# Layer 3's products inside layer 2: source tiles 13 to 48 in batches of eight, 18 dense node tiles, all count matrices made by step 256

## The chip, the cores and the metric

The kernel runs on one core of a Trainium2 chip. The metric is the device time of one execution in microseconds. Before the change it is 3082.79 us, the median of three runs (3079.99 to 3087.31 us). All times below belong to one execution that the hardware profiler recorded; that one took 3087.14 us.

## The reference: what is computed

A graph network of four layers runs over 6,250 nodes with 256 features and 100,000 edges, and its result is added to the input. `src` is random; `dst` is sorted and crowded at low node numbers (the square of a uniform variable), so node 0's neighbourhood has many more edges than node 6,249's.

```
h = relu(layernorm(x))
h = h @ W1_self + mean(h[src] by dst) @ W1_neigh + b1
hp = relu(h @ W2_pool + b2_pool)
h = h @ W2_self + max(hp[src] by dst) @ W2_neigh + b2
h = ((sum(h[src] by dst) + h) / (deg + 1)) @ W3_neigh + b3
h = h @ W4_self + mean(h[src] by dst) @ W4_neigh + b4
out = x + h @ W_fc + b_fc
```

Weight matrices that follow one another are multiplied together in the kernel, so that layers 3 and 4 are sums over edges, with scalings.

## The kernel before, in words

Nodes are cut into 49 tiles of 128 rows (P = 128); edges into T = 782 steps of 128. The work lies in `fast_path`; `general_path` stands behind an `If` that is not taken for these inputs.

**Sums over edges, in two ways.** For node tiles with many edges ("dense" tiles: the first 8 in layer 1, 16 in layer 3, 18 in layer 4; `HUB = (8, 16, 18)`, in the code H1, H3, H4) the kernel has a count matrix: for destination tile d and source tile s, how often each source row reaches each destination row, as fp8 numbers. `dense` (L424) multiplies it with the source rows, which are held as three bf16 parts in turn: three matmuls for each pair (d, s) (L435). For the other node tiles, `sums` (L360) gathers 128 source rows for each edge step by an indirect DMA on GpSimd's queue (L379), and multiplies them with a one-hot matrix (three matmuls, L397). Layer 3 gathers from the edge step at which tile H3 can begin: 342 steps with H3 = 16 (314 with 18, as layer 4 has it). The dense work is handed out evenly over these steps through a `Hub`, a list of work items of which `advance` runs so many.

**Count matrices.** `build` (L291) makes one from 128-edge rows. For each item ScalarE makes one one-hot matrix (two activations, L303 and L305), VectorE another (L307), TensorE multiplies them (L313), ScalarE copies the sum into the tile `A` (L317), of which there is one (`bufs=1`); after each tile's 32 items SyncE writes `A` (784 KB) to the table `tab_a` (L321). Tiles 0 to 7 are made in layer 1, tiles 8 to 17 during layer 2.

**Layer 2** is a running maximum over all 782 edge steps, in six blocks of steps taken from the last to the first (100, 130, 180, 220, 100, 52 steps). Each step: one gather of 128 rows of 2 KB from `tab_p` on GpSimd's queue (L1137), a VectorE maximum with the row before (L1142), for every second step a write of the result to `runb` by SyncE (L1183). In the last three blocks a second maximum merges two rows (L1178), and half as much is written. There are six buffers of two steps each for `X`. At the end of each block `carry` joins the partial maxima across partitions (L1006 to L1040): gather, maximum, scatter; only then are the node tiles of this block finished by `done2` (L1055), from tile 48 down to tile 0, spread over the steps: it gathers the maxima (`totals`, `tot`, at most 4 buffers), waits for four steps, then makes transposes, eight fp32 matmuls (L1070 to L1076), the sum `prf` (L1080), and splits it into three bf16 parts `r3` (L280 to L283), which SyncE writes to `tab_r`, layer 3's table.

**Layer 3's products inside layer 2.** While the parts of tile d are still on chip, the kernel uses them for layer 3's dense sums: `EARLY = (6, 38)` says for which source tiles, `BATCH = 4` how many are taken at once. `early_products` (L1099) makes for each batch and each of the H3 dense tiles one load of the counts (`ae`, 64 KB, SyncE, L1108) and one group of 4 x 3 matmuls of 512 columns into a PSUM bank (`psd`, 2 banks); then `add3` (L931) adds the bank to an fp32 accumulator in SBUF on VectorE (L934; the first time a ScalarE copy, L937). The source tiles outside this range are done in layer 3 from tiles `zt` that are loaded from `tab_r` when that stage opens (`late`, three loads, 17 source tiles).

**The order.** The Python loop at L1128 to L1200 hands out the work step by step (`at` counts the steps): so many builds, so many items of early work, one piece of each open `done2`. Within that order of priority the compiler's scheduler places instructions in each engine's queue; each engine then runs its own queue in order. Builds of tiles 8 to 15 are spread up to step 250, those of 16 and 17 from there to step 682. Early work runs at a fortieth of what is left, rounded up, at each step; tile 37 to 34's batch is the first and is handed over at step 307.

```
early.advance(early.done + math.ceil(early.left() / 40))
if tiles and not ends and begun2 < NT * (at - FIRST_AT) / (T - 20 - FIRST_AT):
```

Of the kernel before, what the change touches and what calls it, by code (L numbers as in the profile page):

```python
# [10 lines left out]
BF16 = mybir.dt.bfloat16  # L11
F16 = mybir.dt.float16
F8 = mybir.dt.float8e4
# [7 lines left out]
P = 128  # L21
# [6 lines left out]
MERGED = 3  # L28
Z_SIGMA = 5.0
WIN = 8  # L30
HUB = (8, 16, 18)
EARLY = (6, 38)
MADE_AT = 64
FIRST_AT = 112
EARLY_AT = 250


def _edges_below(n, E, N):
# [35 lines left out]
def fast_path(  # L74
# [18 lines left out]
    FH = W1_self.shape[1]  # L93
    FO = W_fc.shape[1]
    NT = (N + P - 1) // P
# [3 lines left out]
    T = (E + P - 1) // P  # L99
# [11 lines left out]
    for d in range(NT):  # L111
# [4 lines left out]
        g_of.append((g0, g1))  # L116
    JC = g_of[HUB[0]][0] * G // P
    offs = [0]
# [13 lines left out]

    H1, H3, H4 = HUB
    WT = P // WIN
# [80 lines left out]
    at = 0  # L215
# [110 lines left out]
    LOOK = 4  # L326
# [195 lines left out]
    RB1 = -(-(max(row_of[w, k] for w in range(WT * H1) for k in range(k_of[w])) + 1) // P) * P  # L522
# [275 lines left out]
    with ExitStack() as on:  # L798
# [3 lines left out]
        psb = on.enter_context(tc.tile_pool(name="psb1", bufs=2, space=PSUM))  # L802
        psd = on.enter_context(tc.tile_pool(name="psd1", bufs=2, space=PSUM))
        wk = on.enter_context(tc.tile_pool(name="fl1", bufs=2))
# [4 lines left out]
        def done1(d, acc):  # L809
# [23 lines left out]
            for k in range(KI):  # L833
# [12 lines left out]
                        lambda acc, d=d: todo.append(done1(d, acc)), extra=1)  # L846
                  for d in range(H1)]
        work = list(builds[0])
        first = len(work)
        for d in range(H1):  # L850
            work += merged(denses[d], builds[d + 1]) if d + 1 < H1 else denses[d]
        hub = Hub(work)
# [86 lines left out]
    with tc.tile_pool(name="fl2c", bufs=1) as ck, ExitStack() as late:  # L939
# [3 lines left out]
        psb = late.enter_context(tc.tile_pool(name="psb2", bufs=2, space=PSUM))  # L943
# [4 lines left out]
        skR = ck.tile([P, RB * P - RB1], F32, name="skR")  # L948
        mkR = ck.tile([P, RB * P - RB1], F32, name="mkR")
# [52 lines left out]
        wk = late.enter_context(tc.tile_pool(name="fl2", bufs=2))  # L1002
# [51 lines left out]

        def done2(d):  # L1055
            tots, th = totals(d)
            for _ in range(4):
                yield
            hm = tots[0]
            for t in tots[1:]:  # L1060
                nc.vector.tensor_tensor(hm, hm, t, op=ALU.max)
            yield
            pt = bank(pst, "pt", "pt_hTf", (KH, P))
            for j in range(KH):
                nc.tensor.transpose(pt[:, j, :], hm[:, j * P : (j + 1) * P], ident)
            hT = wk.tile([P, KH, P], F32, name="hTf")
            nc.scalar.copy(hT, pt)  # L1067
            pm = bank(psm, "pm", "pm_prf")
            for k in range(KI):
                nc.tensor.matmul(pm, th[:, k, :], usA[:, k, :], start=(k == 0), stop=False)  # L1070
            yield
            for k in range(KI):
                nc.tensor.matmul(pm, th[:, KI + k, :], usB[:, k, :], start=False, stop=False)
            yield
            for c in range(KH):
                nc.tensor.matmul(pm, hT[:, c, :], un[:, c, :], start=False, stop=(c == KH - 1))  # L1076
                if c == 1:
                    yield
            pr = wk.tile([P, FH], F32, name="prf")
            nc.vector.tensor_add(pr, pm, prow)  # L1080
            yield
            if d < H3:
                add3(d, pr)
            r3 = early_pool[0].tile([P, 3 * FH], BF16, name="r3", bufs=2 * BATCH + 1)
            parts(pr, FH, r3)
            nc.sync.dma_start(tab_r[d * P : (d + 1) * P, :], r3)
            if EARLY[0] <= d < EARLY[1]:
                ready.append((d, r3))
                if len(ready) == BATCH or d == EARLY[0]:
                    early_products()  # L1090
            yield


        BATCH = 4
        ready = []
        early = Hub()
        early_pool = []

        def early_products():  # L1099
            batch = dict(ready)  # L1100
            ss = sorted(batch)
            ready.clear()
            for d in range(H3):
                got = {}

                def load(d=d, got=got):
                    got[0] = early_pool[0].tile([P, BATCH, P], F8, name="ae", bufs=LOOK + 3)
                    nc.sync.dma_start(got[0][:, : len(ss), :].bitcast(BF16),  # L1108
                                      tab_a[d, :, ss[0] : ss[-1] + 1, :])

                work = dense(ss, lambda s, got=got: got[0][:, s - ss[0], :],
                             lambda s: batch[s], FH, psd, lambda v, d=d: add3(d, v))
                early.add([(load, work[0])] + work[1:])
# [2 lines left out]
        todo = [chains(), node_rows(wk, psm)]  # L1116
        steps = products2(wpool)
        A = wk.tile([P, NT, P], F8, name="A", bufs=1)
        first, rest = (
            [w for d in ds for w in build(d, A, (skR, mkR, RB1), wk, psb)]  # L1120
            for ds in (range(H1, H3), range(H3, H4))
        )
        hub = Hub(first + rest)
        tiles, begun2 = [], 0
        ends = []
        now = []
        at = 0
        for b in reversed(range(NB)):  # L1128
            tb = BLOCKS[b]
            t0 = offs[b] // P  # L1130
            prev = None
            for s0 in range(0, tb, G2):
                n = min(G2, tb - s0)
                X = (xmore if at // G2 % 2 else xpool).tile([P, G2, FH], F32, name="X2")
                for k in range(n):
                    t = t0 + s0 + k
                    nc.gpsimd.indirect_dma_start(  # L1137
                        out=X[:, k, :], out_offset=None, in_=tab_p,
                        in_offset=bass.IndirectOffsetOnAxis(ap=srcI[:, t : t + 1], axis=0),
                    )  # L1140
                    if s0 + k:
                        nc.vector.scalar_tensor_tensor(  # L1142
                            X[:, k, :], prev, same[:, t : t + 1], X[:, k, :],
                            op0=ALU.mult, op1=ALU.max,
                        )
                    prev = X[:, k, :]
                    at += 1
                    if at > 8:
                        next(steps, None)
                        if todo and next(todo[0], 0) == 0:  # L1150
                            todo.pop(0)
                    if at == MADE_AT:
                        for _ in steps:
                            pass
                        top.close()
                        early_pool.append(
                            top.enter_context(tc.tile_pool(name="early3", bufs=1)))
                    if at <= EARLY_AT:
                        hub.advance(math.ceil(len(first) * max(0, at - 16) / (EARLY_AT - 16)))
                    else:  # L1160
                        hub.advance(len(first) + math.ceil(
                            len(rest) * (at - EARLY_AT) / (T - 100 - EARLY_AT)))
                    early.advance(early.done + math.ceil(early.left() / 40))
                    if s0 + k > 2 and ends and next(ends[0], 0) == 0:
                        ends.pop(0)
                        tiles += [d for d in reversed(range(NT)) if b_of[d][0] == last_b]
                    if tiles and not ends and begun2 < NT * (at - FIRST_AT) / (T - 20 - FIRST_AT):
                        now.append(done2(tiles.pop(0)))
                        begun2 += 1
                    for g in list(now):  # L1170
                        if next(g, 0) == 0:
                            now.remove(g)
                r0 = s0
                if b < MERGED:
                    r0 = s0 // 2
                    if s0 + n < tb:
                        t = t0 + s0 + 1
                        nc.vector.scalar_tensor_tensor(  # L1178
                            X[:, 0, :], prev, same[:, t : t + 1], X[:, 0, :],
                            op0=ALU.mult, op1=ALU.max,  # L1180
                        )
                        n = 1
                nc.sync.dma_start(  # L1183
                    runs[b][r0 * P : (r0 + n) * P, :].rearrange("(g p) f -> p g f", p=P),
                    X[:, :n, :],
                )
            end = carry(b, prev)
            next(end)
            ends.append(end)
            last_b = b  # L1190
# [49 lines left out]
    with ExitStack() as on:  # L1240
# [2 lines left out]
        psm = on.enter_context(tc.tile_pool(name="psm3", bufs=2, space=PSUM))  # L1243
        zk = on.enter_context(tc.tile_pool(name="fz4", bufs=1))
        Z4 = {}
        z4_early = ((16, 23), (23, 30), (30, 37))
        z4_late = ((0, 7), (7, 14), (14, 16), (37, 44), (44, NT))

        with tc.tile_pool(name="fl3", bufs=2) as wk:
            def done3(d, acc):  # L1250
# [33 lines left out]
                    if d == s1 - 1:  # L1284
                        Z4.update(resident(zk, tab_s, FO, s0, s1))

            late = ((EARLY[1], 44), (44, NT), (0, EARLY[0]))
            Z3 = {}
            for s0, s1 in late:
                Z3.update(resident(wk, tab_r, FH, s0, s1))  # L1290
# [3 lines left out]
            for d in range(H3):  # L1294
                work += dense([s for s0, s1 in late for s in range(s0, s1)], lambda s, d=d: block(d, s), lambda s: Z3[s], FH, psd,
                              lambda acc, d=d: todo.append(done3(d, acc)))
            sums(wk, psg, tab_r, FH, srcE, keyE, jb, H3, done3, 7, Hub(work), wait=14, todo=todo)

        with tc.tile_pool(name="fl4", bufs=2) as wk:
# [15 lines left out]
            for d in range(H4):  # L1315
                work += dense([s for s0, s1 in order for s in range(s0, s1)],
                              lambda s, d=d: block(d, s), lambda s: Z4[s], FO, psd,
                              lambda acc, d=d: todo.append(done4(d, acc)))
# [644 lines left out]
```

## Time and profile before

| | us |
|---|---|
| median of three runs | 3082.79 |
| the profiled execution | 3087.14 |
| its span on the core | 3085.3 |
| start of layer 2's gathers | 821.0 |
| last of layer 2's gathers | 2105.5 |
| last write of `tab_r`, layer 3 opens | 2139.64 |
| loads of `zt` for layer 4, which opens | 2647.1 |

TensorE is busy for 2456.4 us of the span (80%), VectorE 2053.6 (67%), GpSimd 2054.0 (67%), ScalarE 893.7 (29%); the DMA engines move 865.38 MB. Such shares are means over four stages that have different limits; a row of the stage view gives the busy time of each engine (and in brackets its instructions) in one stretch, the share of full clock that TensorE was granted, and the busy share of the 16 DMA engines. A DMA share of about 1 means that they had no free time. A row of a group of instructions gives its line, engine, operands, number, busy time, mean length, and after the bar how long its engine stood idle just before it and for whom. Back-to-back matmuls overlap in their recorded lengths, so their rate is read from a run of several.

### The profile page before, as it was taken

How to read it: one execution, taken by the hardware profiler on the slowest of the kernel's cores; microseconds unless marked ns; L12 is line 12 of the kernel's file. 1: busy time of each engine (PE TensorE's matmuls, PEld its weight loads, DVE VectorE, ACT ScalarE, POOL GpSimd, SP SyncE). 2: the span in 40 equal slices, each digit the busy share in tenths (PEclk: the TensorE clock that was granted, in tenths of full speed). 3: DMA queues.
4: the chain of work that ended last, by engine and by line, in shares of the span. 5: the costliest groups of instructions: out<-in, count | busy, mean ns of one | idle time of the engine just before them, and what ended most of it. 6: DMA issues, size and time to landing. Idle time of an engine off the chain costs nothing. (4 is left out here: it accounts for less than half of the span.)

```text
span 3085.3 us, 41397 instructions
## 1 busy us (share of the span) xinstructions
PE 2456.4 (80%) x12699; PEld 1401.4 (45%) x12699; DVE 2053.6 (67%) x5303; ACT 893.7 (29%) x2383; POOL 2054.0 (67%) x2260
## 2 busy tenths in 40 slices
PE   1568999999768555666789997972899899799997
PEld 0234666666433222232334443431344344688786
DVE  4955666655367677555789997974466667576665
ACT  2557766664255566311111111000000001000000
POOL 5274777776366776777667777764676677677663
PEclk9777999999889777788899998985999999899999
DMA  5454667776599999999989998976999999777774
GB/s 190 152 159 138 203 208 211 213 217 211 196 392 376 362 388 352 362 389 384 314 274 324 315 309 296 323 248 210 361 387 373 364 386 382 254 225 219 208 210 135
DMA packets 379984, 865.38 MB, mean 280 GB/s; under 512 B 58064, under 2 KB 151202, under 8 KB 379720
## 3 DMA queue, kind: packets, MB, share of 16 engines
q0 software_dynamic: 146560, 514.74, 50.7%
q1 hardware_dynamic: 175108, 292.47, 25.6%
q10 hardware_dynamic: 58084, 55.44, 5.6%
q8 instruction: 103, 1.69, 0.2%
q14 instruction: 129, 1.06, 0.1%
HBM read 610.65 MB, written 252.58 MB: 280 GB/s over the span
## 5 line engine op out<-in xcount | busy, mean ns | idle before, releaser
L1137 POOL DMA_INDIRECT X<-tab_p,srcIf x782 | 842.3, 1077 | 368.6 <-issue 170.5
L397 PE MATMUL pg<-ring,hot 128*128 128x256 bf16 (+2 forms) x3390 | 685.9, 311 | 96.2 <-DMA ring<-tab_h,srcT 36.5
L435 PE MATMUL pd<-zt,ac 128*128 128x256 bf16 (+1 forms) x3462 | 569.9, 300 | 36.3 <-DMA ac<-tab_a 31.1
L379 POOL DMA_INDIRECT ring<-tab_h,srcT x474 | 450.7, 951 | 194.3 <-PE pg L397 72.2
L397 PEld LDWEIGHTS <-hot 128*128 128x128 bf16 x3390 | 334.2, 99 | 332.1 <-issue 163.4
L435 PE MATMUL pd<-r,ae 128*128 128x512 bf16 x1536 | 383.4, 399 | 102.9 <-DVE acc L934 46.9
L379 POOL DMA_INDIRECT ring<-tab_r,srcE x342 | 333.0, 974 | 162.2 <-PE pg L397 72.5
L435 PEld LDWEIGHTS <-ac 128*128 128x128 fp8e4 x3462 | 338.8, 98 | 171.3 <-DMA ac<-tab_a 23.9
L379 POOL DMA_INDIRECT ring<-tab_s,srcE x314 | 297.7, 948 | 130.2 <-PE pg L397 49.4
L1142 DVE SCALAR_TENSOR_TENSOR X<-X,samef,X 128x512 f32<-128x512 f32 x385 | 288.3, 749 | 133.2 <-DMA X<-tab_p,srcIf 90.9
L416 DVE SCALAR_TENSOR_TENSOR acc<-pg,M,acc 128x257 f32<-128x257 f32 (+2 forms) x518 | 274.7, 561 | 150.6 <-PE pg L397 150.3
L1142 DVE SCALAR_TENSOR_TENSOR X<-X,samef 128x512 f32<-128x512 f32 x391 | 293.1, 750 | 114.2 <-DMA X<-tab_p,srcIf 108.0
L313 PE MATMUL pb<-hm,hs 128*128 128x392 bf16 x781 | 256.2, 376 | 132.4 <-ACT A L317 66.4
L305 ACT ACTIVATE hs<-ht,onef 128x128 bf16<-128x128 bf16 x781 | 290.2, 395 | 240.9 <-PE pb L313 221.9
L435 PEld LDWEIGHTS <-ae 128*128 128x128 fp8e4 x1536 | 156.4, 102 | 338.9 <-issue 198.8
L1219 DVE TENSOR_SCALAR_CACHE_REDUCE many<-ac 128x896 bf16<-128x896 fp8e4 (+2 forms) x144 | 138.7, 963 | 132.7 <-DMA ac<-tab_a 132.7
L1076 PE MATMUL pm_prf<-unf,hTf 128*128 128x512 f32 x392 | 203.9, 647 | 16.6 <-ACT hTf L1067 16.6
L375 DVE TENSOR_SCALAR hot<-iota_bf,keyE 128x128 bf16<-128x128 bf16 x656 | 151.2, 274 | 72.5 <-PE pg L397 65.4
L307 DVE TENSOR_SCALAR hm<-iota_w,mk 128x392 bf16<-128x392 f16 x461 | 155.2, 344 | 56.7 <-PE pb L313 55.0
L317 ACT ACTIVATE A<-pb 128x392 fp8e4<-128x392 f32 x288 | 139.8, 489 | 182.0 <-PE pb L313 137.7
L435 PE MATMUL pd<-Z,A 128*128 128x256 bf16 (+1 forms) x1176 | 187.4, 274 | 0.2
L313 PEld LDWEIGHTS <-hs 128*128 128x128 bf16 x781 | 81.4, 105 | 217.7 <-issue 89.2
(288 smaller groups left out, 2908.1 us busy)
## 6 DMA issues: line engine op xcount, KB each, us to landing
runb<-X SPq DMA_DIRECT2D x208, 512.0 KB
runb<-X SPq DMA_DIRECT2D x183, 256.0 KB
tab_r<-r SPq DMA_DIRECT2D x49, 384.0 KB
tab_a<-A SPq DMA_DIRECT2D x18, 784.0 KB
tab_t<-th SPq DMA_DIRECT2D x49, 256.0 KB
tab_p<-hpf SPq DMA_DIRECT2D x49, 256.0 KB
th<-tab_t ACTq DMA_DIRECT2D x49, 256.0 KB
X<-tab_p,srcIf POOLq DMA_INDIRECT x782
```

What stands on the lines that cost most here:

```text
L305: nc.scalar.activation(hots[0], t, AF.Relu, bias=one, scale=-1.0)
L307: nc.vector.tensor_scalar(hots[1], iota_w, mk[:, r : r + 1], None, op0=ALU.is_equal)
L313: nc.tensor.matmul(hold[0], hots[0], hots[1], start=(k == 0), stop=(k == k_of[w] - 1))
L317: nc.scalar.copy(A[:, :, c : c + WIN], hold[0].rearrange("p (s c) -> p s c", c=WIN), saturate=True)
L375: nc.vector.tensor_scalar(hot[j], iota_b, keyT[:, j - jb : j - jb + 1], None, op0=ALU.is_equal)
L379: nc.gpsimd.indirect_dma_start(out=ring[:, j % deep, : 3 * F], out_offset=None, in_=table, in_offset=bass.IndirectOffsetOnAxis(ap=srcT[:, ...
L397: nc.tensor.matmul(pg[:, : F + c], hot[j], X[:, part * F : (part + 1) * F + c], start=(k == 0 and part == 2), stop=(k == n - 1 and part == 1),
L416: nc.vector.scalar_tensor_tensor(acc[d], pg, m, acc[d], op0=ALU.mult, op1=ALU.add)
L435: nc.tensor.matmul(hold[0][:, : F + c], a, z[:, part * F : (part + 1) * F + c], start=(s == ss[0] and part == 2), stop=(s == ss[-1] and pa ...
L1076: nc.tensor.matmul(pm, hT[:, c, :], un[:, c, :], start=False, stop=(c == KH - 1))
L1137: nc.gpsimd.indirect_dma_start(out=X[:, k, :], out_offset=None, in_=tab_p, in_offset=bass.IndirectOffsetOnAxis(ap=srcI[:, t : t + 1], axis=0),
L1142: nc.vector.scalar_tensor_tensor(X[:, k, :], prev, same[:, t : t + 1], X[:, k, :], op0=ALU.mult, op1=ALU.max,)
```

## The change

The dense tiles of layer 3 become 18. The early products take source tiles 13 to 48, in batches of eight, and start after step 236, by a thirtieth of what is left. All ten count matrices of layer 2 are made by step 256. `done2` waits eight steps instead of four for its gathered maxima. The buffers of `r3` become 16 (from 9), those of `ae` 6 of 128 KB (from 7 of 64 KB). In layer 3 the source tiles 0 to 12 are left for `zt`, in two loads. The loads of layer 4's table are cut at other tiles.

```diff
-HUB = (8, 16, 18)
-EARLY = (6, 38)
+HUB = (8, 18, 18)
+EARLY = (13, 49)
-EARLY_AT = 250
+MADE_BY = 256
+EARLY_AT = 236
...
-            for _ in range(4):
+            for _ in range(8):
                 yield
...
-            r3 = early_pool[0].tile([P, 3 * FH], BF16, name="r3", bufs=2 * BATCH + 1)
+            r3 = early_pool[0].tile([P, 3 * FH], BF16, name="r3", bufs=2 * BATCH)
...
-        BATCH = 4
+        BATCH = 8
...
-                    got[0] = early_pool[0].tile([P, BATCH, P], F8, name="ae", bufs=LOOK + 3)
+                    got[0] = early_pool[0].tile([P, BATCH, P], F8, name="ae", bufs=LOOK + 2)
...
-        hub = Hub(first + rest)
+        hub = Hub([w for d in range(H1, H4) for w in build(d, A, (skR, mkR, RB1), wk, psb)])
...
-                    if at <= EARLY_AT:
-                        hub.advance(math.ceil(len(first) * max(0, at - 16) / (EARLY_AT - 16)))
-                    else:
-                        hub.advance(len(first) + math.ceil(
-                            len(rest) * (at - EARLY_AT) / (T - 100 - EARLY_AT)))
-                    early.advance(early.done + math.ceil(early.left() / 40))
+                    hub.advance(math.ceil(len(hub.work) * max(0, at - 16) / (MADE_BY - 16)))
+                    if at > EARLY_AT:
+                        early.advance(early.done + math.ceil(early.left() / 30))
...
-        z4_early = ((16, 23), (23, 30), (30, 37))
-        z4_late = ((0, 7), (7, 14), (14, 16), (37, 44), (44, NT))
+        z4_early = ((18, 25), (25, 32), (32, 39))
+        z4_late = ((0, 7), (7, 14), (14, 18), (39, 45), (45, NT))
...
-            late = ((EARLY[1], 44), (44, NT), (0, EARLY[0]))
+            late = ((0, 7), (7, EARLY[0]))
```

More of the change, by code (lines that the diff above doesn't have):

```diff
@@ L1118, in fast_path @@
         A = wk.tile([P, NT, P], F8, name="A", bufs=1)
[L1119 to L1122, printed above, removed]
-        hub = Hub(first + rest)
+        hub = Hub([w for d in range(H1, H4) for w in build(d, A, (skR, mkR, RB1), wk, psb)])
         tiles, begun2 = [], 0
```

## The prediction, made before the changed kernel was built or run

> **What bounds the kernel now.** I read the stage view first, cut at layer 2's blocks and at layer 3; then, for pace, the same view for layer 2's gathers alone (L1137); then waits, groups, time line and chain in the stretches that the change touches.
>
> All instructions by stage:
> ```profile
> core 0: us, PE busy (x) PEld busy (x) DVE busy (x) ACT busy (x) POOL busy (x), PEclk, DMA share, GB/s
> 821.00:1203.00 382.00, 246.37 (x733) 121.21 (x734) 259.62 (x656) 216.49 (x637) 261.65 (x252) 0.80 1.01 374
> 1203.00:1487.00 284.00, 189.73 (x585) 82.70 (x585) 169.05 (x282) 75.21 (x194) 202.70 (x190) 0.80 1.01 375
> ...
> 1600.00:1860.00 260.00, 244.07 (x943) 111.31 (x942) 244.21 (x380) 48.66 (x108) 198.41 (x179) 0.99 0.94 317
> ...
> 1900.00:2000.00 100.00, 97.49 (x371) 44.18 (x370) 96.69 (x145) 10.24 (x17) 77.34 (x73) 1.00 0.97 329
> ```
> L1137 alone:
> ```profile
> 1203.00:1487.00 284.00, 185.01 (x173) 0.80 1.01 375
> ...
> 1600.00:1860.00 260.00, 187.91 (x169) 0.99 0.94 317
> ...
> 1900.00:2000.00 100.00, 71.08 (x67) 1.00 0.97 329
> ```
> Layer 2 has two halves. Up to 1487 us (step 410, where merged blocks begin) DMA is full (1.01): 284/173 = 1.64 us a step, whatever the engines do. After it VectorE (94%), TensorE (94%) and DMA (0.94) are all nearly full at 260/169 = 1.54 us a step. In 1900 to 2000, without builds, a step takes 100/67 = 1.49.
>
> Layer 3, same view, and its chain:
> ```profile
> 2200.00:2620.00 420.00, 391.98 (x1773) 173.00 (x1772) 288.09 (x715) 37.23 (x92) 301.19 (x309) 0.99 1.00 377
> ```
> ```profile
> 2562.12 0.65 PE pd L435 x3
> 2562.77 0.65 PE pg L397 x3
> 2563.41 0.65 PE pd L435 x3
> ```
> DMA is at 1.00 and TensorE at 93%, here unbroken in the chain; three matmuls take 0.65 us.
>
> Waits in 1600 to 2110, and groups in 1937 to 1997:
> ```profile
> DVE tot L1061 <- DMA tot<-runb,rows_of: 18.1, 3, 11.6
> ...
> PE pd L435 <- DVE acc L934: 16.8, 16, 5.7
> ...
> DVE acc L934 <- PE pd L435: 1.2, 4, 0.6
> ```
> ```profile
> L1137 POOL DMA_INDIRECT X<-tab_p,srcIf x42 | 45.7, 1089 | 13.3 <-issue 10.4 <-DMA runb<-X 1.2 <-DVE X L1178 1.1
> L435 PE MATMUL pd<-r,ae 128*128 128x512 bf16 x184 | 42.2, 379 | 1.6 <-DVE acc L934 1.6
> ```
> VectorE hardly waits for early products (1.2 us). At 1937 to 1997 a backlog of 94 early items (64 new, 30 left) was handed out at three a step; TensorE was full, yet a step took 60/42 = 1.43 us. The gathers outran a late TensorE.
>
> **Layer 3, part by part.** It loses 342 - 314 = 28 gather steps. Dense products go from 16 x 17 x 3 = 816 to 18 x 13 x 3 = 702 matmuls; own products (`pm_own`) from 33 to 31 tiles, 6 matmuls. Three prices:
> - TensorE: (84 + 114 + 6) x 0.216 = -44 us.
> - GpSimd: 28 issues of 0.95 and 0.30 us between them = -35 us.
> - DMA: 28 x 393 KB at 377 GB/s = -29 us. Against it, tiles 38 to 48 are no longer resident: 9 more `zown` loads (+3.5 MB), four tiles less of `zt` (-1.6 MB), 234 instead of 272 count blocks of 16 KB (-0.6 MB): +1.3 MB, +3.5 us. Together -26 us.
>
> DMA is the fullest, and what saves least decides: -26. At the opening the chain has a wait of 31 us for the later `zt` loads, and steps around 2174 to 2196 take 2.2 us instead of 1.3. The second load now ends after 5.1 MB, not 6.7: -6 to -9 us. The first is larger (2.75 for 2.36 MB in 14.6 us: +2 us), and the last tiles now wait for a `zown` load on SP's queue behind `tab_s` writes: 0 to +5, I take +2. Sum about **-30 us**, from -22 to -44.
>
> **Layer 4** has the same 314 gathers, 18 dense tiles and 28 late tiles; the third early load starts at tile 38 instead of 36. 0, from -3 to +5.
>
> **Layer 2: builds by step 256.** Tiles 16 and 17 move here: 64 items (128 activations, 64 VectorE masks, 64 matmuls, 32 copies) and two 784 KB `tab_a` writes, which on SP's queue come between `runb` writes. The work itself hides: ScalarE is busy for 216 of 382 us, and 64 items at about 0.78 us (starts 0.295 us apart for each activation, half a copy of 0.38) add 50. The bytes do not hide: 1.6 MB at 375 GB/s = 4 us. Each tile end also makes ScalarE wait for the write of the single `A`, 43.6 us for seven; two more, 12 us, if that reaches the gathers through VectorE's masks. I take **+4**, range 0 to +16.
>
> **Early products, steps 237 to 410.** Before, they begin at step 307. Now batches 48 to 41 and 40 to 33 fall here: 18 x 16 = 288 pairs (d, s), 864 matmuls, in place of some 110 pairs. DMA is full, so the extra `ae` loads, (288 - 110) x 16 KB = 2.9 MB, cost **+8 us**. Whether TensorE falls behind hangs on its clock. An item is 0.65 us and a finished tile 8.0 (16 fp32 records at 0.43, transposes 1.1):
> ```profile
> 1591.98 0.81 PE L435 MATMUL pd<-r,ae 128*128 128x512 bf16 x3
> 1592.63 1.88 PE L1076 MATMUL pm_prf<-unf,hTf 128*128 128x512 f32 x4
> 1594.34 0.81 PE L435 MATMUL pd<-r,ae 128*128 128x512 bf16 x3
> ```
> At full clock this half asks 288 x 0.65 + 13 x 8.0 = 291 us of TensorE, in 284. The row grants 0.80, which makes it 364, 80 us late. The Trainium skill (TensorE: Matmul & The Clock Gate, Part 1: The HAM clock gate) says that idleness throttles the clock and some 3.4 us of steady work releases it. The rows agree: 0.80 at 67% busy, 0.99 at 94%. I take 0.95 (306 us, 22 late): lateness goes into the next half, where such backlogs did not hold the gathers. From both sides: 0 to +40.
>
> **From step 410.** VectorE is relieved: 90 bank sums instead of 128, fewer still in this half because two batches are done before; about 0.16 additions and 0.17 masks less a step, 0.16 x 0.68 + 0.17 x 0.34 = 0.17 us of its 1.45 busy. Next late is DMA: 1.54 x 0.94/1.01 = 1.43 us. TensorE still asks 360 items x 0.65 + 27 x 8.0 = 450 us (plus lateness) of about 620, but mostly before step 660; so I go half way, to 1.48. Over the 315 of the 372 steps outside block ends: **-19 us**, from 0 (TensorE takes VectorE's place) to -35.
>
> Is TensorE full there? The skill (Perfetto Trace Analysis, Identifying the Most-Contended Engine) calls matmul occupancy a poor measure and names weight-load time instead: 111 of 260 us, 43%, so the 408 added matmuls (88 us) would be free. By count, 1700 to 1860 us holds 423 early matmuls (92 us), 114 fp32 records (49), and some 12 of builds and transposes: 153 of 160 us. I follow the count; by the rule I would take 1.43, 16 us more gain.
>
> **Small parts.** Eight waits instead of four: the 18.1 us of waiting for `tot` could shrink, but gathers of `X` queue behind `tot` on GpSimd, so VectorE would mostly wait for them; buffers are held 6 us longer of 20 between tiles. -18 to +5, taken 0. Groups of 24 matmuls save TensorE part of its 16.8 us waits for `add3`; 16 `r3` buffers hold exactly two batches, and a late batch holds up ScalarE's copies: together 0. The tail from 2105.5 to 2139.64 (carry, tile 0) stays.
>
> Sum: +4 + 8 - 19 - 30 = **-37 us**. Against the profiled execution's 3087.1 (1.8 us outside its span) that is 3050; it stands 4.3 us over the median, so I forecast **3046**.
>
> **Rivals.**
> - *Bursts hold VectorE (slower), 3105 us.* A batch now hands out 5, 4, 3, 2, 1 items a step: 5, 8, 9 and 15 steps cost TensorE 3.8, 3.2, 2.5 and 1.9 us with `done2`, 96 us against 37 x 1.54 = 57. If VectorE's `add3` (L934) stands early in its queue, the maxima of L1142 behind it wait, then `X` buffers, gathers and DMA. Twelve buffered steps cover 18 of the 39 us; 20 are lost per full batch. Two bursts in the DMA-bound half give +40, and the fall of 19 fails: 12 + 40 - 30 = +22. All four would give 3145. It decides from about 9 us of waiting per batch. For: batches are twice as large and meet the builds' end. Against: 1.2 us of such waits before, and the 1.43 at 94 items.
> - *Given back, 3077 us.* Builds cost their 12, loads 8, TensorE takes VectorE's place (0), layer 3 gives 26.
> - *More than forecast, 3002 us.* The second half runs at DMA's 1.43 (-35), waits for `tot` go (-18), layer 3 gives -40; costs 12.
> - That early products are not moved can be excluded: batch one is complete at step 218, its counts for the first 16 tiles too by then or soon after.
>
> **How the numbers follow.** Forecast 0.50 (own range 3025 to 3070), bursts 0.26, given back 0.13, more 0.11. About 0.2% (6 us) can be told from no change. Faster: 0.50 + 0.11 + half of given back = 0.67; same: the rest of it and a little of the bursts, 0.08; slower 0.25. The range 3005 to 3112 leaves out most of the 3145 case and half of the best.
>
> **What would show it.** Right: 314 gathers in layer 3, its stage shorter by about 30 us and DMA still at 1.0; early products from about 1200 us; a clock over 0.9 and DMA 1.0 in 1203 to 1487; 1.48 us a step later, VectorE below 90%, almost no early work at the end. Wrong: waits of VectorE for L435 or `prf` above 30 us, or DMA falling below 0.95 before step 410; a step staying at 1.54; a layer 3 that keeps its length because `zown` loads come late.

## The result and the profile after

The changed kernel takes 3227.38 us (median of four runs, 3224.13 to 3233.18); the kernel before took 3085.05 beside it. The ratio is 1.0469, 95% interval [1.0444, 1.0495]. The forecast was 3046. The profiled execution's span is 3227.6 us, 142 more than before.

| stretch, us (layer 3: number of gathers in brackets) | before | after | difference | forecast |
|---|---|---|---|---|
| layer 2's gathers, steps 0 to 236 | 377 | 377 | 0 | +4 |
| steps 236 to 410 | 287 | 291 | +4 | +8 |
| steps 410 to 781 | 620 | 692 | +72 | -19 |
| last gather of layer 2 to first of layer 3 ("tail") | 37 | 139 | +102 | 0 |
| layer 3's gathers | 476 (342) | 438 (314) | -38 | -30 |
| from there to layer 4's first gather | 18 | 27 | +9 | 0 |
| layer 4 to the end | 449 | 442 | -7 | 0 |

In the changed file `add3`'s addition on VectorE is L935 (before L934), its ScalarE copy L938, the early matmuls L436, the maximum L1139, the node products L1071 to L1077, `prf` L1081. The stage view of the changed kernel, all instructions; columns as in the prediction:
```profile
core 0: us, PE busy (x) PEld busy (x) DVE busy (x) ACT busy (x) POOL busy (x), PEclk, DMA share, GB/s
1203.00:1487.00 284.00, 191.31 (x664) 84.52 (x665) 162.77 (x292) 92.25 (x256) 192.77 (x180) 0.83 0.99 360
1600.00:1860.00 260.00, 214.60 (x784) 95.43 (x784) 205.13 (x303) 17.83 (x30) 181.00 (x168) 0.92 0.88 285
...
2100.00:2182.00 82.00, 61.77 (x225) 25.94 (x226) 47.75 (x70) 4.01 (x7) 24.52 (x26) 0.88 0.54 164
2182.00:2320.00 138.00, 113.69 (x333) 53.33 (x331) 49.79 (x99) 21.27 (x36) 21.40 (x22) 0.91 0.32 102
2400.00:2740.00 340.00, 308.44 (x1364) 133.06 (x1363) 228.64 (x576) 30.77 (x76) 238.36 (x244) 0.97 1.00 382
```
Up to 1487 us DMA is full as before. From 1600 to 1860 nothing is full any more: VectorE is down from 94% to 79%, as the forecast wished, but DMA falls too, from 0.94 to 0.88. In the rows 2100 to 2182 and 2182 to 2320 no resource but TensorE is over 60%; the second is the tail, with DMA at 0.32. Its groups:
```profile
L1077 PE MATMUL pm_prf<-unf,hTf 128*128 128x512 f32 x96 | 47.9, 640 | 0.7 <-ACT hTf L1068 0.7
...
L436 PE MATMUL pd<-r,ae 128*128 128x512 bf16 x69 | 15.5, 379 | 0.6 <-DVE acc L935 0.6
...
L1081 DVE TENSOR_TENSOR prf<-pm_prf,prowf 128x512 f32<-128x512 f32 x12 | 8.3, 691 | 45.3 <-PE pm_prf L1077 45.3
```
Twelve tiles are finished behind the last gather (`prf` x12, and the 96 records of L1077 are eight for each); before it was one. TensorE is busy for 114 of the tail's 138 us. So the question is why the finishing came so late. Counted in the traces, by step of layer 2's gathers:

| by step | 236 | 300 | 410 | 500 | 640 | 700 | last |
|---|---|---|---|---|---|---|---|
| tiles finished, before | 8 | 14 | 19 | 27 | 37 | 43 | 48 |
| tiles finished, after | 5 | 9 | 13 | 17 | 27 | 32 | 37 |
| early matmuls begun, before | 0 | 0 | 288 | 576 | 1152 | 1323 | 1536 |
| early matmuls begun, after | 0 | 147 | 408 | 744 | 1215 | 1388 | 1875 |

The forecast had 864 early matmuls and 21 tiles done by step 410. It got 408 and 13.

Waits of the changed kernel in 1203 to 2181 us (total, times, longest):
```profile
ACT r L281 <- DVE prf L1081: 533.6, 30, 62.6
...
PE pd L436 <- DVE acc L935: 78.7, 26, 12.1
...
PE pd L436 <- ACT acc L938: 47.5, 3, 23.0
...
DVE acc L935 <- PE pd L436: 5.2, 4, 2.5
...
DVE prf L1081 <- PE pm_prf L1077: 1.7, 1, 1.7
```
VectorE hardly waits for TensorE (5.2 and 1.7 us). TensorE waits for VectorE and ScalarE. In 1203 to 1490 us, where it ought to have got ahead, these are its longest waits:
```profile
PE pd L436 <- ACT acc L938: 42.2, 2, 23.0
PE pb L314 <- DVE hm L308: 22.8, 8, 4.5
PE pb L314 <- ACT A L318: 17.1, 5, 5.3
```
The first is for a bank that ScalarE has to copy, the others are for the builds' masks and copies. The longest single wait in the time line, with all engines:
```profile
1385.80 1.88 PE L1077 MATMUL pm_prf<-unf,hTf 128*128 128x512 f32 x4
...
1387.51 5.34 PE L436 MATMUL pd<-r,ae 128*128 128x512 bf16 x24
...
1397.09 0.75 DVE L1139 SCALAR_TENSOR_TENSOR X<-X,samef 128x512 f32<-128x512 f32 x1 [3.73 <-DMA X<-tab_p,srcIf]
...
1412.30 0.68 DVE L1081 TENSOR_TENSOR prf<-pm_prf,prowf 128x512 f32<-128x512 f32 x1
1413.02 0.62 ACT L281 CAST r<-prf 128x512 bf16<-128x512 f32 x1 [36.46 <-DVE prf L1081]
...
1415.24 0.58 ACT L938 COPY acc<-pd 128x512 f32<-128x512 f32 x1
1415.87 1.44 PE L436 MATMUL pd<-r,ae 128*128 128x512 bf16 x3 [23.01 <-ACT acc L938]
```
The products that `prf` needs are done by 1387.7 us. `prf` comes 24 us later, and in between VectorE does 13 maxima and stands idle for gathers, as at 1397.09: `prf` is behind those maxima in its queue. ScalarE's queue has the split of `prf` (L281) ahead of the copy of a full bank (L938), and TensorE waits for that bank. A late piece of VectorE's queue thus turns into idle time of TensorE.

The order of that queue is set when the kernel is compiled. In the compiled queue of VectorE one tile's `prf` lies behind the last maximum before the change, and twelve after it. Run and compiled order agree, so the tail is no accident of timing.

### The profile page after: what moved, and what is told of

It reads as the page before. It is cut to its first block, busy times and chain, and to the rows that moved or that the text cites. A ratio compares the mean times of both kernels' runs of the same rounds, so it can differ in the third digit from the quotient of the medians.

```text
span 3227.6 us, 41650 instructions
## 1 busy us (share of the span) xinstructions
PE 2534.8 (79%) x12903; PEld 1430.4 (44%) x12903; DVE 2022.3 (63%) x5222; ACT 890.5 (28%) x2385; POOL 2023.1 (63%) x2232
## 5 line engine op out<-in xcount | busy, mean ns | idle before, releaser
L398 PE MATMUL pg<-ring,hot 128*128 128x256 bf16 (+2 forms) x3306 | 663.4, 310 | 103.7 <-DMA ring<-tab_r,srcE 40.3
L436 PE MATMUL pd<-r,ae 128*128 128x512 bf16 x1944 | 484.1, 405 | 148.7 <-DVE acc L935 79.3
L436 PE MATMUL pd<-zt,ac 128*128 128x256 bf16 (+1 forms) x3348 | 542.7, 298 | 33.8 <-DMA ac<-tab_a 31.2
L398 PEld LDWEIGHTS <-hot 128*128 128x128 bf16 x3306 | 325.2, 99 | 333.7 <-issue 173.2
L1139 DVE SCALAR_TENSOR_TENSOR X<-X,samef,X 128x512 f32<-128x512 f32 x385 | 288.6, 750 | 221.5 <-DMA X<-tab_p,srcIf 174.7
L1139 DVE SCALAR_TENSOR_TENSOR X<-X,samef 128x512 f32<-128x512 f32 x391 | 293.7, 751 | 176.0 <-DMA X<-tab_p,srcIf 164.7
L380 POOL DMA_INDIRECT ring<-tab_r,srcE x314 | 307.0, 978 | 151.0 <-PE pg L398 65.7
L436 PEld LDWEIGHTS <-ae 128*128 128x128 fp8e4 x1944 | 200.1, 103 | 451.7 <-issue 269.0
L436 PEld LDWEIGHTS <-ac 128*128 128x128 fp8e4 x3348 | 330.3, 99 | 154.0 <-issue 25.7
L417 DVE SCALAR_TENSOR_TENSOR acc<-pg,M,acc 128x257 f32<-128x257 f32 (+2 forms) x505 | 266.1, 556 | 134.1 <-PE pg L398 133.5
L1077 PE MATMUL pm_prf<-unf,hTf 128*128 128x512 f32 x392 | 204.8, 655 | 39.0 <-ACT hTf L1068 39.0
L281 ACT CAST r<-prf 128x512 bf16<-128x512 f32 x49 | 30.3, 618 | 572.0 <-DVE prf L1081 563.1
L436 PE MATMUL pd<-Z,A 128*128 128x256 bf16 (+1 forms) x1176 | 187.1, 273 | 0.2
```

The source lines that it names most:

```text
L380: nc.gpsimd.indirect_dma_start(out=ring[:, j % deep, : 3 * F], out_offset=None, in_=table, in_offset=bass.IndirectOffsetOnAxis(ap=srcT[:, ...
L398: nc.tensor.matmul(pg[:, : F + c], hot[j], X[:, part * F : (part + 1) * F + c], start=(k == 0 and part == 2), stop=(k == n - 1 and part == 1),
L417: nc.vector.scalar_tensor_tensor(acc[d], pg, m, acc[d], op0=ALU.mult, op1=ALU.add)
L436: nc.tensor.matmul(hold[0][:, : F + c], a, z[:, part * F : (part + 1) * F + c], start=(s == ss[0] and part == 2), stop=(s == ss[-1] and pa ...
L1139: nc.vector.scalar_tensor_tensor(X[:, k, :], prev, same[:, t : t + 1], X[:, k, :], op0=ALU.mult, op1=ALU.max,)
```

## Experiments

Theories, as the expectations name them. A: buffers of the finishing work (`th2`, `tot`) and its eight waits hold tiles back. B: bursts alone delay it. C: TensorE has no time for early products and finishing where the change puts them. D: only the compiled order of VectorE's queue is bad. E: the prediction's rival, bursts hold VectorE. F: loads and sums, not matmuls. The runs e1 to e8 were made on chips on which the kernel before takes 3459 to 3462 us, mostly because its other layers are longer there (layer 2 starts at 1048 us); ratios and lengths of stages are compared. "Layer 2 with tail" is the time from layer 2's first gather to layer 3's first: 1322 before, 1499 after (1518 for the changed kernel with four waits on those chips, 1374 for the kernel before with eight).

**e1, four waits again.**
```diff
-            for _ in range(8):
+            for _ in range(4):
```


> The changed kernel with four waits in done2 instead of eight. Theory A (finished tiles fall behind because a tile's two th2 buffers are held too long, and the longer wait is a good part of the holding): first tiles finish some 20 steps earlier, fewer than 13 tiles are left after the last gather, tail shorter than 138 us; total 3150 to 3200. Theory B (bursts of early products alone hold up done2): no more than 10 us from the 3227 of the changed kernel. Theory C (TensorE has too much work in layer 2): no change.

1.0305 [1.0273, 1.0337]; tail 143 us, 12 tiles; layer 2 with tail is 1518, as in e2, which has eight waits (1516). The waits have no part in it.

**e2, more buffers.** `th2` 4 instead of 2, `tot` 5 instead of 4, `r3` 14 instead of 16 to make room.

> The changed kernel with four th2 buffers instead of two, five tot instead of four, and 14 r3 instead of 16 to make room. Theory A: tiles no longer queue for th2; the tail after the last gather falls from 138 us to below 70 us and the total to 3130 or less. Theory C (too much TensorE work): total stays within 20 us of 3227. If tot, not th2, is the short buffer, a small gain of under 30 us.

1.0312 [1.0280, 1.0344]; tail 138 us, 12 tiles. Theory A falls.

**e3, no early products at all.** Layer 3's dense sums lack source tiles 13 to 48.
```diff
-            for d in range(H3):
+            for d in range(0):
```


> The changed kernel with the early products left out altogether (layer 3's dense sums miss source tiles 13 to 48): no ae loads, no 1944 matmuls, no bank sums; done2, builds and the rest as they are. If the bursts cause the lag (A or B): done2 keeps pace, tail 37 us as before the change, gathers end at 2105 or earlier, total 3000 to 3050. If the eight waits or the faster builds cause it: a tail of well over 37 us remains, total above 3100.

0.9759 [0.9724, 0.9793]; tail 38 us, 1 tile. By step 300 it is as late as the changed kernel (9 tiles), but it has 22 at step 410 and 37 at 500. With the builds at their old place (e4) 14 tiles are done by step 300; with the builds moved and no early product yet (e5), 9. So the builds make the first lag, and without early products it is made good.

**e4, the kernel before with eight waits.** The edit of e1 the other way round.

> The kernel before with eight waits in done2 instead of four, nothing else. If the longer hold of th2 matters by itself (A): done2 lags, 3110 to 3160. If it matters only together with bursts: within 15 us of 3083. If the wait helps, as the prediction allowed: down to 3070.

0.9971 [0.9943, 0.9998]; tail 38 us. No loss; if anything, a gain of 0.3%.

**e5 and e6, halves of the change.** e5 is the kernel before with 18 dense tiles and all matrices by step 256; e6 is the kernel before with tiles 13 to 48 in batches of eight from step 237, and 16 dense tiles. Each has 1728 early matmuls. Buffers and later loads are changed to suit, which the cuts below leave out.
```diff
-HUB = (8, 16, 18)
+HUB = (8, 18, 18)
...
-EARLY_AT = 250
+EARLY_AT = 256
```
```diff
-EARLY = (6, 38)
+EARLY = (13, 49)
...
-        BATCH = 4
+        BATCH = 8
...
-                    early.advance(early.done + math.ceil(early.left() / 40))
+                    if at > 236:
+                        early.advance(early.done + math.ceil(early.left() / 30))
```


> The kernel before with 18 dense tiles in layer 3 and all ten count matrices by step 256; source tiles 6 to 37 in batches of four as before. Theory D (VectorE's queue is written with the finishing work of a tile behind too many maxima, so that tiles are left after the last gather): the compiled queue has 4 tiles behind the last maximum, tail 60 to 70 us, layer 3 some 25 us shorter, total within 15 us of before. Theory C (TensorE has no time for the added products): 288 pairs less of work than in the changed kernel, no tail of note, total 20 to 30 us below before.

> The kernel before with source tiles 13 to 48 in batches of eight from step 237 at a thirtieth; 16 dense tiles and builds as before. Theory D: the compiled queue has 6 tiles behind the last maximum, tail 75 to 95 us; layer 3 keeps its 342 gathers and loses only its dense products (192 matmuls), 0 to 15 us; total 30 to 60 us above before. Theory C: about the same stage times but TensorE near full in the second half.

1.0095 [1.0058, 1.0132] and 1.0119 [1.0078, 1.0160]; tails 88 and 71 us, with 4 and 6 tiles behind the last maximum. Layer 2 with tail is 1433 and 1408. Each half is enough to start the loss. The compiled queue had announced the tiles; theory C, which expected e5 to come out 20 to 30 us ahead, missed.

**e7, gathers held back.** The changed kernel with 8 gathers of buffers for `X` instead of 12 (the second pool has 1 pair instead of 3).

> The changed kernel with four pairs of X buffers instead of six (xrows2 has one instead of three), nothing else. The compiled queue then has 1 tile behind the last maximum instead of 12, with the same instructions. Theory D: tail back to about 40 us and total at least 70 us below the changed kernel's 3227, unless eight gathers ahead are too few for the DMA queues. Theory C (too much TensorE work): gathers end later by what the tail loses, total stays at about 3227.

1.229 [1.2248, 1.2332]. The tail is gone (38 us), but a step takes 2.7 us in steps 0 to 236 (646 us) and the run tells nothing of C against D.

**e8, a milder version.** The kernel before with 18 dense tiles and matrices by step 300, tiles 6 to 37 in fours, and the finishing of tiles paced to end 80 steps earlier.
```diff
-HUB = (8, 16, 18)
+HUB = (8, 18, 18)
...
-EARLY_AT = 250
+EARLY_AT = 300
...
-                    if tiles and not ends and begun2 < NT * (at - FIRST_AT) / (T - 20 - FIRST_AT):
+                    if tiles and not ends and begun2 < NT * (at - FIRST_AT) / (T - 100 - FIRST_AT):
```


> The kernel before with 18 dense tiles in layer 3, all ten count matrices by step 300 (not 256), source tiles 6 to 37 in batches of four as before, and done2 started a little earlier from tile to tile (T - 100 in place of T - 20). Compiled queue: 2 tiles behind the last maximum. Theory D: tail 45 us, layer 3 some 25 us shorter, total 10 to 30 us below before. If layer 3's saving is not real: as before.

0.9961 [0.9939, 0.9983]; tail 49 us. It is ahead of the kernel before by some 0.4%; of the versions that compute the whole result only e4, with 0.3%, is ahead too.

**e9 to e12, VectorE held in the order of the loop.** From here on the kernel before takes 3083 to 3085 us. A directive around layer 2's loop keeps VectorE's instructions in the order in which Python hands them out; the other engines are ordered by the compiler as always.
```diff
+        with tc.manual_schedule(engines={mybir.EngineType.DVE}):
             for b in reversed(range(NB)):
...
```


> The changed kernel with VectorE's instructions of layer 2 held in the order in which the loop hands them out, so that no maximum overtakes the finishing work or a bank sum; the other engines stay as the compiler orders them. In the compiled queue of VectorE 1 tile's finishing stands behind the last maximum instead of 12; instructions and buffers are the same. Theory D (the order of VectorE's queue makes the tail, TensorE has the time): tail about 40 us, at least 60 us below the changed kernel, at most 1.02 of the kernel before. Rival E (the prediction's: bursts of eight hold VectorE): with the order held VectorE waits for the bank sums and the finishing, over 60 us in all, the gathers take longer by what the tail gains, 1.03 or more.

> The kernel before with VectorE held in the loop's order in the same way: what the hold itself costs. Both theories: between 1.00 and 1.03 of the kernel before, tail unchanged at about 37 us.

> The version with 18 dense tiles, matrices by step 300, tiles 6 to 37 in batches of four (0.9961 of the kernel before), with VectorE held in the loop's order. Theory D: its tail goes from 49 to about 40 us, 0.98 to 1.00. Rival E: the hold costs more than the tail gives, above 1.01.

> The changed kernel itself on this chip, beside the three others. All theories: gathers end 70 to 80 us later than in the kernel before, a tail of about 140 us with 12 tiles finished after the last gather, 1.03 to 1.05.

Changed kernel held: 1.0497 [1.0462, 1.0533], tail 38 us, but the gathers take 1485 us instead of 1354 in e12. Kernel before held: 1.0248 [1.0218, 1.0277]. e8 held: 1.0505 [1.0466, 1.0544], against an expectation of at most 1.00; why it loses twice what e10 loses was not taken apart. Changed kernel again: 1.0442 [1.0408, 1.0476], tail 139 us. Theory D in its plain form falls: the right order took the tail away and gave nothing back. But the hold lengthens the gathers of the kernel before by 90 us, 79 of them in steps 0 to 236 (456 against 377), so a cleaner pair was needed.

**f1 to f4.** The hold begins at step 257. In f3 and f4 only one of the three bf16 parts of the early products is multiplied, 648 matmuls instead of 1944, so layer 3's sums lack the other two; loads, bank sums and order of work stay.
```diff
+                    if at == 257:
+                        held.enter_context(tc.manual_schedule(engines={mybir.EngineType.DVE}))
...
```
```diff
-                              lambda s: batch[s], FH, psd, lambda v, d=d: add3(d, v))
+                              lambda s: batch[s], FH, psd, lambda v, d=d: add3(d, v), ps=(2,))
...
```


> The changed kernel with VectorE held in the loop's order only from step 257 on, when the count matrices are made. The hold of the whole stage cost 80 us in steps 0 to 236, in the kernel before too; those should be gone. Theory D (only the order of VectorE's queue was bad, TensorE has the time for early products and finishing): tail about 40 us, gathers end within 20 us of the same hold in the kernel before, total at most 1.00 of the kernel before. Theory C (TensorE does not have the time where the change puts the work; the compiler's order only chose where that shows): tail about 40 us too, but the gathers from step 236 on take 70 to 110 us longer than in the kernel before with the hold, VectorE waits over 100 us for L436 and for the node products, total 1.02 to 1.04.

> The control: the kernel before with the same hold from step 257 on. Both theories: 0.99 to 1.01, tail 37 us.

> The changed kernel with the hold from step 257 on and a third of the matmuls of the early products: of the three bf16 parts only one is multiplied, so layer 3's sums of source tiles 13 to 48 lack the other two for the dense tiles. Loads, bank sums and order of work stay. Theory C: the gathers end within 20 us of the control's, total 0.97 to 1.00, below the control by about layer 3's 30 us. Theory D: no different from the run with all matmuls, within 1%. Rival F (the loads of the counts or the bank sums delay the gathers, not matmuls): no different either, 1.02 to 1.04.

> The changed kernel without any hold, with a third of the matmuls of the early products as in f3. In the compiled queue of VectorE 1 tile's finishing now stands behind the last maximum, as against 12. Theory C: the tail is 40 us, the gathers end by 2120 us or its like on this chip, total 0.97 to 1.00. Rival F: the gathers still end 60 us or more later than in the kernel before.

| | ratio, interval | gathers | tail | layer 3 |
|---|---|---|---|---|
| f1 changed, held | 1.0490 [1.0457, 1.0523] | 1473 | 38 | 442 |
| f2 before, held | 1.0091 [1.0061, 1.0121] | 1309 | 36 | 476 |
| f3 changed, held, a third | 1.0061 [1.0042, 1.0079] | 1344 | 37 | 438 |
| f4 changed, free, a third | 0.9882 [0.9851, 0.9913] | 1280 | 38 | 440 |

f4 against the changed kernel (1360 + 139 us): 1296 matmuls with their weight loads fewer, every other instruction the same, though ordered anew by the compiler, and layer 2 with tail is 181 us shorter. It then lies within 4 us of the kernel before. Theory F falls. Waits of VectorE behind step 236, of f1, f2 and f3 in turn:
```profile
DVE prf L1082 <- PE pm_prf L1078: 102.2, 20, 28.9
DVE acc L936 <- PE pd L437: 86.6, 34, 6.3
```
```profile
DVE prf L1081 <- PE pm_prf L1077: 41.0, 15, 7.4
...
DVE acc L935 <- PE pd L436: 10.9, 13, 3.6
```
```profile
DVE prf L1082 <- PE pm_prf L1078: 48.9, 13, 15.9
...
DVE acc L936 <- PE pd L437: 2.2, 1, 2.2
```
With the order held, lateness can't move to the end, so VectorE waits for TensorE: 189 us in f1 against 52 in the control. A third of the matmuls brings that back to 51, and the gathers are 129 us shorter, with VectorE's order that of the loop from step 257 on in both. So f4's gain does not come from a new order alone. Such waits are those of the prediction's rival, bursts that hold VectorE; in the changed kernel the compiler's order has the late pieces behind the maxima, and the time is lost at the end.

f1's gathers lose more than C expected (164 us against the control, not 110). f3 missed too: its gathers end 33 us later than the control's, not within 20, and its total is only 9 us below. Part of that is the hold itself; stage rows for steps 236 to 270, of f1, f2 and f3:
```profile
1196.00:1350.00 154.00, 128.19 (x484) 58.43 (x483) 59.49 (x149) 91.39 (x262) 42.53 (x42) 0.91 0.53 186
```
```profile
1199.00:1275.00 76.00, 52.78 (x130) 22.02 (x131) 46.68 (x101) 45.83 (x135) 43.77 (x41) 0.75 0.93 328
```
```profile
1198.00:1322.00 124.00, 96.06 (x312) 43.06 (x311) 59.94 (x150) 88.64 (x261) 42.10 (x42) 0.86 0.67 230
```
In f3 these 34 steps still take 48 us more than in the control, with ScalarE busy for 89 us: builds that were handed out by step 256 but not done. The hold makes the maxima wait for them; under the compiler's order the changed kernel takes 66 us for these steps. Behind step 270 the gathers take 945 us in f1, 857 in f2 and 843 in f3: 88 us more than the control with all matmuls, 14 less with a third.

**f5 and f6, amount or place.** The changed kernel with source tiles 20 to 48 early, 1566 matmuls; f6 also makes the matrices by step 300 and hands out early work from step 291.
```diff
-EARLY = (13, 49)
+EARLY = (20, 49)
...
```


> The changed kernel with source tiles 20 to 48 done early instead of 13 to 48: 29 x 18 x 3 = 1566 matmuls of early products inside layer 2, about the 1536 of the kernel before; start, batches of eight, dense tiles and builds as changed, no hold. Tiles 13 to 19 go to layer 3, which should take 30 to 50 us more than in the changed kernel. In the compiled queue of VectorE 6 tiles' finishing stands behind the last maximum. If the amount of TensorE's early work alone is at fault: steps 236 to 781 within 20 us of the kernel before, tail at most 50 us. If its place is at fault too (first batch in the builds' end, finishing put back by the bursts): a tail of 70 to 100 us all the same.

> f5 with the count matrices made by step 300 instead of 256 and the early products handed out from step 291 instead of 237, so that fewer of them stand in front of the first tiles' finishing. Compiled queue: 3 tiles behind the last maximum. If only the amount counts: as f5. If the place counts: tail shorter than f5's by 20 us or more, total 0.99 to 1.00 of the kernel before.

1.0282 [1.0244, 1.0320] and 1.0157 [1.0110, 1.0204]; tails 69 and 57 us; layer 2 with tail 1394 and 1370, layer 3 479 and 473. Of the 177 us that layer 2 with tail lost, 105 come back with the amount, 24 more with the place, 48 remain. Both matter; both expectations missed in size (f5's tail lies between its two cases, at most 50 and 70 to 100; f6's was to be 20 us shorter than f5's and is 12, and its total was to reach 1.00).

## Why the prediction was wrong

**Right, or near it.** Builds +4: steps 0 to 236 did not change (377 us), but the builds are done later than handed out, as said under f3, and they set the finishing back, 5 tiles by step 236 instead of 8. Early products up to step 410, +8: +4, which is luck, as less than half of them were done by then. Eight waits, 0: e1 and e4. Layer 3, -30: -38 for 28 gathers less, DMA at 1.00. Layer 4, 0: -7, but 9 more in front of it. f4, which has all of the change but two thirds of the early matmuls, stands at -36 us against the kernel before (0.9882); the forecast was -37. That they meet so closely is partly luck: f4's steps 236 to 410 took 15 us more than before, not 8, and its layer 3 took 36 less, not 30. But the lines beside TensorE's work were about right.

**The step that failed: "lateness goes into the next half, where such backlogs did not hold the gathers".** Two things were wrong in it: how late TensorE would be, and where its lateness would be paid.

The first is the size. At a clock of 0.95 the forecast had TensorE 22 us late at step 410. The clock was 0.83 in 1203 to 1487 us, at 67% busy, as it had been 0.80 at 67% before; and what was done by step 410 falls short by (864 - 408)/3 = 152 items of 0.65 us and 8 tiles of 8.0 us: 99 + 64 = 163 us. The larger part isn't the clock: 291 us of work at 0.83 are 351 us, which would be 67 us late. TensorE was busy for only 191 of 284 us, no more than the 190 before the change. It stood idle since its work hung on VectorE's and ScalarE's queues: the three waits of 1203 to 1490 us make 82 of its 93 idle us, and the time line at 1387 to 1416 us shows one of them. So the spare time of this row could not be filled with work that takes many steps on several engines. A step ahead of it failed as well: the prediction held that batch one is complete at step 218, but by step 236 only 5 of its 8 tiles were done, and the first early matmul began at 1268 us, not about 1200.

The second is where lateness ends. From step 410 the forecast asked 450 us of TensorE in 620. With what was left over it had (1944 - 408)/3 = 512 items and 36 tiles: 333 + 288 = 621 us in 620, and no slack. That VectorE's gathers outran a late TensorE was read rightly from the 94 items of backlog, but those were 60 us of a backlog that was worked off before the end. Here it was not: 12 tiles and 69 early matmuls, 12 x 8.0 + 69 x 0.216 = 111 us of TensorE, were left behind the last gather, since work that the maxima don't need, finishing and bank sums, stood behind the last maximum. "The tail stays" was then wrong by 102 us. By this sum the work would just have fitted. It did not, since TensorE stood idle here too: in the stage view it is busy for 546 of the 695 us from 1487 to 2182, and nearly all of its 79 us of waits for bank sums in VectorE's queue (L935) lie here. The same sum for other runs, from their counts at step 410:

| | asked from step 410, us | of 620 | layer 2 with tail, against 1322 |
|---|---|---|---|
| f4 | 398 x 0.216 + 31 x 8.0 = 334 | 54% | -4 |
| before | 416 x 0.65 + 30 x 8.0 = 510 | 82% | 0 |
| f6 | 384 x 0.65 + 33 x 8.0 = 514 | 83% | +48 |
| f5 | 386 x 0.65 + 36 x 8.0 = 539 | 87% | +72 |
| after | 512 x 0.65 + 36 x 8.0 = 621 | 100% | +177 |

The order is right, but the share does not give the size: the kernel before and f6 ask almost the same, and f6 loses 48 us. On the chips of e1 to e8, where these steps take 658 us in e4, the order holds as well: e4 78%; e8 and e6 both 83%, with 8 and 34 us more than e4; e5 90% and 59; e1 95% and 144. So a kernel at some 80% stands close to where the loss begins, and where the work lies decides the rest. Such an agreement is no proof; that the matmuls are the cause is shown by f4, and by f3 against f1.

**The rival "bursts hold VectorE"** was right that late TensorE work would cost time, and wrong on the place: 6.9 us of such waits in the changed kernel, where it asked for over 30, and 189 us only when the order is held. Its number was too small as well: 3227 lies 82 us above its case of four bursts, 3145, and the range ended at 3112. "Forecast", "given back" and "more" all took TensorE's added 88 us as hidden or as a bound of the pace; none let them add to the end.

**Weight loads or occupancy.** In place of matmul occupancy the Trainium skill (Perfetto Trace Analysis, Identifying the Most-Contended Engine) gives two measures: MFU, the floating-point work done as a share of the peak, and the share of time in weight loads. The prediction named the second alone and set its count of matmuls against it; the count is closer to the first. Following the count was right: the 1600 to 1860 row shows weight loads for 95 of 260 us, 37%, which would leave ample room, in a layer whose length f4 shows to hang on TensorE's matmuls.

**Open.** Of the 72 us that steps 410 to 781 lost, 55 lie behind step 720 (164 us instead of 108), where a step takes 2.7 us while DMA is at 0.54. Bank sums lie between the maxima there, and the gathers wait for maxima and writes to free `X`. In f4 these steps take 99 us and in f1 101, so the loss goes with late matmuls under the compiler's order; how it arises was not taken apart. Nor was the compiled order of the changed kernel tried with fewer matmuls: f4's smaller load also changes the order (1 tile behind the last maximum). And why f6, with a sum like that of the kernel before, still loses 48 us is not known.

## What to carry to other kernels

Before filling a stage's idle engine, sum what the engine must do from there to the stage's end, at the clock that the row shows, with every tile that is still unfinished: here a demand of 82% of the time left did no harm in the kernel before, 83% cost 48 us in f6 and 87% cost 72 us in f5. Part of the time left can't be filled where the work hangs on other engines' queues: here TensorE was late and yet busy for only 546 of 695 us. A backlog that does no harm in the middle of a stage is not free: follow what it delays to the last instruction, and ask what the next stage waits for. And look at the compiled queue of the engine that carries the chain: how many pieces of finishing work stand behind the chain's last link tells of a tail before anything runs, if only roughly (4 tiles and 88 us in e5, 6 and 71 in e6).

## What was not expected of the hardware

With buffers for 8 gathers instead of 12 (e7) a step took 2.7 us instead of 1.6 in steps 0 to 236. The same kernel took 12% longer on other chips (3460 us). Most of the 375 us lies outside layer 2: by e4's trace layer 2 began at 1048 instead of 821 us, layer 4 took 504 instead of 449, layer 3's gathers 506 instead of 476.
